# Attention with exponentials interleaved in SBUF: the two terms of a chunk alternate in pairs of queries instead of single queries

## The chip, the cores and the metric

The kernel runs on one NeuronCore of a Trainium2 chip. The metric is the device time of one execution in microseconds (us). Three timed executions of the kernel before gave 4507.30, 4506.31 and 4498.84 us; their median is 4506.31 us. Engines are named as in the profile: PE (TensorE), ACT (ScalarE), DVE (VectorE), POOL (GpSimd) and SP (SyncE, which issues most DMAs).

## What is computed

The input is two images of 256 channels on 64 x 64 positions, so 4096 tokens each. The reference has two layers. The first is a state-space block with an MLP (group norm, projections, a causal convolution, a scan over the tokens, an MLP); the change doesn't touch it. The second is an attention layer with eight heads of 32 channels over all 4096 tokens:

```python
qkv = jnp.einsum('bchw,oc->bohw', x, qkv_w) + qkv_b[None, :, None, None]
qkv = qkv.reshape(b, 3, num_heads, head_dim, n)
q, k, v = (qkv[:, 0], qkv[:, 1], qkv[:, 2])
attn_logits = jnp.einsum('bhci,bhcj->bhij', q, k) * scale
attn_weights = jax.nn.softmax(attn_logits, axis=-1)
out = jnp.einsum('bhij,bhcj->bhci', attn_weights, v)
...
x = x + _L1_conv_ref(_gn(x), L1_conv_qkv_w, L1_conv_qkv_b, 8)
```

Everything is float32. The kernel takes the exponentials without subtracting a maximum, and it divides by their sum at the end of each query tile. (A second, slower routine, `attention_any_range`, is run only if a sum has left the range of the numbers; here it is not run.)

## The kernel before, in words

The first layer fills roughly the first half of the span: a planner (`Plan`) orders its instructions by costs and due times. The attention that follows has an order written out by hand, in `attention`, and the change lies there alone.

**Tiles and slots.** Two images are worked one after the other. An image has two groups of four heads, a group has eight tiles of T = 512 queries, and a tile goes over the 4096 keys in NC = 32 pieces of P = 128 keys. One piece of one tile is a slot `s`; there are 2 x 2 x 8 x 32 = 1024 of them. The keys lie on the 128 partitions, the queries along the free axis. In a slot four things happen:

- `logits` (L1120 to L1134): PE makes the logits of four heads, two heads ("a half") per PSUM tile `s` of 128 x 1024; there are three such tiles.
- `exponentials` (L1136 to L1145): ACT takes the exponential of each half from PSUM to SBUF, 1024 elements per partition.
- `values` (L1155 to L1167): PE multiplies the exponentials with the values `v` and adds the product into the PSUM tile `po`. Each head takes a quarter of the array's columns. A float32 product is two matmul instructions, so that a slot has eight here.
- `add_up` (L1169 to L1194): the exponentials are also summed over the keys, for the softmax's divisor. Summing over the 32 slots is elementwise; only at the end of a tile does PE sum over the 128 partitions (`finish`, L1212).

`run` (L1231 to L1262) puts these in this order for slot `s`: the exponentials of `s`, the values of `s - 1`, a piece of the side work (`finish` of the tile before), the logits of `s + 1`, the sums of `s`. So PE's queue alternates between four logit matmuls and eight value matmuls. ACT's queue alternates between the two halves.

**How the sums are shared out.** Half 1 of every slot goes to a tile `e` of its own, contiguous, and is added by POOL (L1185, L1192, L1194) and partly by DVE (L1189, L1191). Half 0 of every slot but the tile's last one goes into a *chunk*, which takes several slots' terms, and DVE sums them with one `tensor_reduce` (`sum_chunk`, L1151 to L1153). A chunk has four places. `place(c)` says where piece `c` goes: the first chunk of a tile takes pieces 0 to 3; every later one takes three pieces in places 1 to 3, and its place 0 has the running sum, which the reduce of the chunk before it wrote there (L1177, L1178). That makes nine such reduces in a tile, and a tenth one (L1175), for pieces 28 to 30, writes the total to `acc_sb`. The last piece's half 0 goes to a contiguous `e` (L1143). Chunks come from a pool of two buffers.

**The chunk's layout, which the change is about.** Per partition a chunk is `[2 q, 2 h, T, 2 k]` in float32. Place `p` is `q = p // 2` and `k = p % 2`, `h` is the head within the half. So for one head and one `q`, the words in memory are: query 0 term k=0, query 0 term k=1, query 1 term k=0, query 1 term k=1, and so on. 16 bytes hold two queries of two terms. Three instructions touch it:

- ACT's exponential (L1144) writes one word, skips one, writes one.
- PE's value matmul (L1161) reads one word, skips one, reads one: 512 words at a step of 8 bytes.
- DVE's reduce (L1153) reads for each query two neighbouring words (k = 0, 1), then two neighbouring words 8 KB further on (q = 1), and writes one word: 4096 words in, 1024 out. For a running sum its output goes to every second word of the next chunk.

The chunk's tiles are also used as plain 2 x 1024 buffers when the second image is projected (L1023 to L1030).

## Time and profile before

| What | Value |
|---|---|
| Timed executions | 4498.84 to 4507.30 us, median 4506.31 us |
| Profiled execution, span from first to last instruction | 4505.2 us |
| Mean granted TensorE clock in it | 0.977 of full speed |
| Busy share of the span | PE 94%, DVE 86%, POOL 85%, ACT 84% |
| First value matmul of the attention to the last (L1161) | about 2119 to 4484 us |

The span is what is seen of the profiled execution; no other time is given for it. It is 1.1 us below the median of the timed ones. A profile line for a group of instructions has: source line, engine, operation, `output<-inputs` by the program's names, shapes, the count after an x, then the busy time of all in us, the mean of one in ns, then the idle time of that engine just before them, and what ended that wait. `PEld` is the loading of weights, which goes on beside the matmuls. "The chain that ended last" follows the program back from its last instruction, at each step to what released it.

### The profile page before, as it was taken

Reading aid. Unit: us, or ns where it says so; the run is one execution under the profiler, and the core shown is the slowest. Engines: PE = TensorE matmul, PEld = TensorE weight load, DVE = VectorE, ACT = ScalarE, POOL = GpSimd, SP = SyncE. Lnnn points to the kernel's source line nnn. Section 1 sums busy time; section 2 is a strip of 40 time slices with the busy share of each in tenths; the row PEclk is TensorE's granted clock in tenths of the full one; section 3 lists DMA queues with packets and bytes.
Section 4 is the critical chain, followed back from the end, with each engine's and each line's share of the span. In section 5 each row is a group of like instructions: output and inputs, shape, how many; then the busy total and the mean of one; then the engine's idle time right before and its main releaser. Section 6 shows DMA issues by size and latency. Waiting matters only on the chain.

```text
span 4505.2 us, 53942 instructions
## 1 busy us (share of the span) xinstructions
PE 4257.1 (94%) x18530; PEld 1642.2 (36%) x18530; DVE 3890.9 (86%) x3309; ACT 3768.4 (84%) x4842; POOL 3807.4 (85%) x2249
## 2 busy tenths in 40 slices
PE   5789999999999999988999999999999999999998
PEld 2233333333333333333333333333353333333333
DVE  4999999999999989894888888888848888888888
ACT  4788888888788889873999999999849999999997
POOL 2999999999999999994788888888728888888886
PEclk8899999999999999999999999999999999999999
DMA  5233333333443434445210140101091110401100
GB/s 192 94 120 101 110 125 122 127 127 127 143 148 134 139 126 140 147 153 144 58 27 17 29 101 17 26 17 30 24 265 35 46 26 17 101 17 29 27 19 8
DMA packets 172281, 389.23 MB, mean 86 GB/s; under 512 B 23392, under 2 KB 49760, under 8 KB 163808
## 3 DMA queue, kind: packets, MB, share of 16 engines
q1 hardware_dynamic: 171120, 383.37, 27.4%
q8 instruction: 147, 2.41, 0.2%
q10 hardware_dynamic: 880, 2.36, 0.2%
q14 instruction: 134, 1.10, 0.1%
HBM read 292.33 MB, written 93.32 MB: 86 GB/s over the span
## 4 chain that ended last, share of the span: by engine, by line
PE 57%; DVE 4%; ACT 3%; POOL 3%; issue 2%; DMA 1%; DVEq 0%; POOLq 0%; SPq 0%; ACTq 0%
PE s L1131 25%; PE po L1161 24%; PE mm L444 3%; DVE h L839 2%; POOL h L845 2%; ACT da L828 1%; ACT L244 1%; PE mm L677 1%; PE s L1016 1%; PE y L871 1%; POOL dbu L834 1%; PE sums_ps L1212 1%; DVE bn L834 1%; PE mm L641 0%; PE bn L444 0%
## 5 line engine op out<-in xcount | busy, mean ns | idle before, releaser
L1153 DVE TENSOR_REDUCE chunk<-chunk 128x1024 f32<-128x4096 f32 x288 | 1270.6, 4412 | 242.4 <-ACT chunk L1144 242.3
L1194 POOL TENSOR_TENSOR acc_p<-acc_p,e 128x1024 f32<-128x1024 f32 x480 | 1151.9, 2400 | 196.7 <-ACT e L1144 178.0
L1144 ACT ACTIVATE chunk<-s 128x1024 f32<-128x1024 f32 x992 | 1121.5, 1131 | 185.5 <-PE s L1131 139.9
L845 POOL TENSOR_TENSOR h<-h,c 128x1024 f32<-128x1024 f32 x512 | 1208.5, 2371 | 42.0 <-ACT state L842 28.9
L1131 PE MATMUL s<-q,k 128*128 128x512 f32 x4096 | 1228.4, 422 | 5.8 <-ACT chunk L1144 4.9
L1161 PE MATMUL po<-chunk,v 128*32 128x512 f32 x3968 | 1121.7, 642 | 0.0
L1161 PE MATMUL po<-e,v 128*32 128x512 f32 x4224 | 1080.0, 605 | 0.0
L1144 ACT ACTIVATE e<-s 128x1024 f32<-128x1024 f32 x1056 | 1072.7, 1019 | 7.4 <-PE s L1131 6.9
L1131 PEld LDWEIGHTS s<-q,k 128*128 128x128 f32 x4096 | 691.3, 188 | 1014.4 <-issue 915.0
L828 ACT ACTIVATE da<-dt_rep,neg_a 128x512 f32<-128x512 f32 x1024 | 690.5, 701 | 128.7 <-DVE h L839 106.0
L1192 POOL TENSOR_TENSOR acc_p<-acc_p,e 128x512 f32<-128x512 f32 x480 | 620.2, 1292 | 129.3 <-ACT e L1144 106.6
L839 DVE TENSOR_TENSOR_SCAN h<-da,state,dbu 128x512 f32<-128x512 f32 x512 | 650.5, 1273 | 42.8 <-POOL dbu L834 40.2
L839 DVE TENSOR_TENSOR_SCAN h<-da,state,bn 128x512 f32<-128x512 f32 x512 | 647.1, 1264 | 11.6
L834 POOL TENSOR_TENSOR dbu<-dtu_rep,b 128x512 f32<-128x512 f32 x384 | 488.5, 1283 | 19.7 <-DMA dtu_rep<-dtu_dram 15.0
L244 ACT ACT_TABLE_LOAD x332 | 426.0, 1283 | 6.7 <-PEq L1451 0.7
L444 PE MATMUL bn<-proj,pick 112*128 112x512 f32 x512 | 296.4, 595 | 112.2 <-DVE h L839 111.6
L871 PE MATMUL y<-h,sum 128*32 128x512 f32 x2048 | 359.1, 635 | 42.2 <-POOL h L845 42.1
L834 DVE TENSOR_TENSOR bn<-dtu_rep,bn 128x512 f32<-128x512 f32 x512 | 348.6, 681 | 41.4 <-PE bn L444 27.8
L1191 DVE TENSOR_TENSOR acc<-acc,e 128x512 f32<-128x512 f32 x448 | 310.7, 694 | 30.9 <-ACT e L1144 17.5
L1161 PEld LDWEIGHTS po<-chunk,v 128*32 128x32 f32 x3968 | 144.3, 108 | 361.5 <-issue 349.9
L444 PE MATMUL mm<-yn,w_in 128*128 128x512 f32 x512 | 254.7, 625 | 10.3 <-ACT yn L534 9.1
L444 PE MATMUL mm<-yn,w 128*128 128x512 f32 x512 | 246.5, 611 | 4.2 <-ACT hid L666 2.1
(143 smaller groups left out, 4016.3 us busy)
## 6 DMA issues: line engine op xcount, KB each, us to landing
dt_rep<-dt_dram SPq DMA_DIRECT2D x128, 512.0 KB, 5.1
dtu_rep<-dtu_dram SPq DMA_DIRECT2D x128, 512.0 KB, 5.7
k<-qk_dram SPq DMA_DIRECT2D x62, 512.0 KB, 7.3
q<-qk_dram SPq DMA_DIRECT2D x124, 256.0 KB, 4.7
b<-bc_dram SPq DMA_DIRECT2D x64, 256.0 KB, 3.0
c<-bc_dram SPq DMA_DIRECT2D x64, 256.0 KB, 3.7
dt_dram<-dt SPq DMA_DIRECT2D x64, 256.0 KB, 2.0
dtu_dram<-lw SPq DMA_DIRECT2D x64, 256.0 KB, 2.3
```

What stands on the lines that cost most here:

```text
L244: self.nc.scalar.preload_act_table_set(self.TABLES[task.table])
L444: nc.tensor.matmul(out, lhsT=lhsT, rhs=rhs, start=(i == 0), stop=(i == len(pairs) - 1))
L828: nc.scalar.activation(da[j].tile, dt.tile[:, j, :], AF.Exp, scale=scale)
L834: engine.tensor_mul(out.tile, dtu.tile[:, j, :], rows.tile)
L839: nc.vector.tensor_tensor_scan(h.tile[:, j, :], da[j].tile, dbu.tile, initial, ALU.mult, ALU.add)
L845: nc.gpsimd.tensor_tensor(h.tile, h.tile, rows_c.tile.unsqueeze(1).to_broadcast([P, 2, T]), ALU.mult)
L1131: nc.tensor.matmul(ps[:, j, :], lhsT=keys[i // NT, kt][:, h, kj : kj + P], rhs=queries[i][:, h, :], start=True, stop=True)
L1144: nc.scalar.activation(e, todo[s].s[half], AF.Exp, scale=SCALE)
L1153: nc.vector.tensor_reduce(out, terms, AX.XY, ALU.add)
L1161: nc.tensor.matmul(tiles[i].po[h * D : (h + 1) * D, :], lhsT=v[:, c, g * P + h * D : g * P + (h + 1) * D], rhs=todo[s].e[h // 2][:, h % 2, :],
L1192: nc.gpsimd.tensor_add(acc_p[:, 1, :], acc_p[:, 1, :], eb[:, 1, :])
L1194: nc.gpsimd.tensor_add(acc_p, acc_p, eb)
```

## The change

The chunk becomes `[2 q, 2 h, T/2, 2 k, 2 u]`, where `u` is the query within a pair. The words of one head and one `q` are now: query 0 term k=0, query 1 term k=0, query 0 term k=1, query 1 term k=1, then the next pair of queries. The same 16 bytes hold the same four values; the middle two have changed places.

```diff
     def chunk():
-        return ec.tile([P, 2, 2, T, 2], F32, name="chunk")
+        return ec.tile([P, 2, 2, T // 2, 2, 2], F32, name="chunk")
...
-        halves = chunk().rearrange("p q h t k -> p q (h t k)").rearrange("p q (m t) -> p q m t", t=T)
+        halves = chunk().rearrange("p q h t k u -> p q (h t k u)").rearrange("p q (m t) -> p q m t", t=T)
...
-                e = todo[s].chunk[:, k // 2, :, :, k % 2]
+                e = todo[s].chunk[:, k // 2, :, :, k % 2, :]
+                logit = todo[s].s[half].rearrange("p h (t u) -> p h t u", u=2)
             else:
                 e = ep.tile([P, 2, T], F32, name="e")
-            nc.scalar.activation(e, todo[s].s[half], AF.Exp, scale=SCALE)
+                logit = todo[s].s[half]
+            nc.scalar.activation(e, logit, AF.Exp, scale=SCALE)
...
         def sum_chunk(s, out):
-            terms = todo[s].chunk.rearrange("p q h t k -> p (h t) q k")
+            terms = todo[s].chunk.rearrange("p q h t k u -> p (h t) u q k")
             nc.vector.tensor_reduce(out, terms, AX.XY, ALU.add)
...
-                sum_chunk(s, tile_.acc[:, 0:2].rearrange("p h t -> p (h t)"))
+                sum_chunk(s, tile_.acc[:, 0:2].rearrange("p h (t u) -> p (h t) u", u=2))
             elif place(c) == 3:
                 todo["chunk"] = chunk()
-                sum_chunk(s, todo["chunk"].rearrange("p q h t k -> p q (h t) k")[:, 0, :, 0])
+                sum_chunk(s, todo["chunk"].rearrange("p q h t k u -> p q (h t) k u")[:, 0, :, 0])
```

So ACT writes two neighbouring words and skips two, PE reads two neighbouring words and skips two, and the reduce reads, for each query, two words 8 bytes apart (k = 0, 1), then two words 8 bytes apart in the other `q`; its outputs for two queries lie side by side. The value matmul's line itself (`todo[s].e[h // 2][:, h % 2, :]`) is unchanged; it follows the new shape of `e`.

## The prediction, made before the changed kernel was run

> **What bounds the kernel now.** I read the costliest groups first, to find the three instructions that touch a chunk, then the chain that ended last, then busy time by window, then the waits. The groups:

> ```profile
> L1153 DVE TENSOR_REDUCE chunk<-chunk 128x1024 f32<-128x4096 f32 x288 | 1270.6, 4412 | 242.4 <-ACT chunk L1144 242.3
> L1144 ACT ACTIVATE chunk<-s 128x1024 f32<-128x1024 f32 x992 | 1121.5, 1131 | 185.5 <-PE s L1131 139.9
> L1161 PE MATMUL po<-chunk,v 128*32 128x512 f32 x3968 | 1121.7, 642 | 0.0
> L1161 PE MATMUL po<-e,v 128*32 128x512 f32 x4224 | 1080.0, 605 | 0.0
> L1144 ACT ACTIVATE e<-s 128x1024 f32<-128x1024 f32 x1056 | 1072.7, 1019 | 7.4 <-PE s L1131 6.9
> ```

> Two pairs of rows do the same arithmetic and differ in the step of the operand in SBUF. An exponential into a chunk (every second word) takes 1131 ns, into the contiguous `e` 1019. A value matmul that reads a chunk takes 642 ns, one that reads `e` 605. The reduce takes 4412 ns for 4096 words, 1.08 ns a word all in. PE's value matmuls were idle before themselves for 0.0 us.

> The chain of waits in a piece of the attention, with start, length and what ran:

> ```profile
> 2544.99 1.13 PE s L1131 x4
> ...
> 2547.17 1.13 PE s L1131 x4
> 2548.30 1.06 PE po L1161 x6
> 2549.36 1.13 PE s L1131 x4
> 2550.49 0.99 PE po L1161 x8
> 2551.48 1.13 PE s L1131 x4
> ```

> The chain has nothing but PE in it: four logit matmuls, then the value matmuls, without a gap. A slot is the distance from one `s` row to the next. From 2544.99 to 2549.36 there are two slots of 2.185 us. The next, to 2551.48, takes 2.12. It is the slot whose value matmuls are of a tile's last piece, where both halves are contiguous (the row has eight, and 0.99 in place of 1.06). So PE pays 0.065 us in each slot that reads a chunk. That is the only price of the old layout that lies on the path.

> How near the others are, over two tiles (64 slots); columns are the window and busy us (count) for PE, weight loads, DVE, ACT and POOL, then clock and DMA:

> ```profile
> 2341.60:2483.00 141.40, 141.40 (x785) 53.77 (x784) 123.78 (x73) 129.35 (x129) 117.92 (x64) 1.00 0.09 23
> ```

> A tile takes 70.7 us and PE is busy in all of it (31 x 2.185 + 2.12 + 0.86 for the sums at its end, by the chain, is 70.7). DVE is busy 61.9 of it, ACT 64.7, POOL 59.0. And the waits of an attention stretch:

> ```profile
> DVE chunk L1153 <- ACT chunk L1144: 107.9, 90, 3.4
> ...
> ACT chunk L1144 <- PE s L1131: 65.3, 314, 1.0
> ```

> DVE waits for ACT, ACT for PE: both follow PE's pace. DVE has 70.7 - 61.9 = 8.8 us free per tile; over ten reduces that is 0.88 us each. A reduce may grow to 4.41 + 0.88 = 5.29 us before DVE sets the pace.

> [...] with two words per line ACT pays (1131 - 1019) / 1024 = 0.11 ns a word and PE 65 / 1024 = 0.06 ns a column (two rounds of 512 in a slot).

> [...]

> [...]

> **The change, part by part.** Comparing the two built programs, every engine has the same instructions in the same order with the same semaphores. Nothing is added, removed or moved, no queue is passed and no wait is added. Only the patterns of 992 exponentials, 3968 matmuls and 320 reduces (288 + 32 a tile's last) differ. So the sum has three terms.

> *ACT's write.* Two adjacent words, then two skipped. The number of 16-byte lines is the same (512), the number of 8-byte units is halved. Best case 1019 ns, a gain of 112 ns x 992 = 111 us of ACT[...]. On the path either is worth nothing: ACT waits for PE ahead of chunk writes (139.9 us in all). The cover is 70.7 - 64.7 = 6.0 us a tile, 0.19 us per chunk write. Value: 0.

> *PE's read.* Same pattern, 256 lines a matmul as before. If PE's price comes with each 8-byte unit, it goes: 0.065 x 992 = 64.5 us gained. If it comes with each line, it stays: 0. [...] One number speaks for the line. In the first layer 16 contiguous float32 matmuls of 512 columns follow one another in 6.87 us (the chain's `mm L677 x16`), 0.84 ns a column; with PE's 0.06 that is 1.80 ns for a line with two words. An exponential of 512 contiguous words takes 588 ns (L600), one of 1024 takes 1019, so 0.84 ns a word and 157 ns of start-up; a chunk write then has (1131 - 157) / 512 = 1.90 ns for a line. [...] I take 0 and keep both ends.

> *DVE's read.* Now no two consecutive words are adjacent: word 0, word 2, a hop of 8 KB, word 0, word 2. By lines nothing changes[...] And ACT and PE, taking single words at 8 bytes' step, lose 7 to 13%[...]. I take 4.41[...]. Its writes (now side by side) are one word in four read and can't matter.

> Sum: 0 + 0 + 0. Against the profile's own span of 4505.2 that is 4505.2; the timed median is 1.1 us higher. Forecast **4506 us**, by itself 4497 to 4517 (the lower edge is the bound of no change[...]).

> **The rivals.**

> *PE is relieved* (faster). PE's price belongs to 8-byte units; slots fall to 2.12. For it: PE is the bound and nothing else is within 6 us a tile; then ACT's 64.7 and DVE's 61.9 still fit under 68.7. Against it: the equal figure per line. Time: 4506 - 64.5 = 4442, or between the two if a part stays.

> *The reduce becomes the bound* (slower). The place is L1153 and the price is the loss of adjacency in its reads; it decides from 5.29 us per reduce. [...] The chunks' two buffers carry it on: a slow reduce holds its chunk, behind it in DVE's queue stand the sums of L1191 and the end of a tile, ACT's next chunk waits for the buffer, and PE for ACT. [...] Both effects could meet: PE relieved and DVE at about 5.1 would still gain the whole 64 us.

> *The change does nothing of what it says* is excluded by the built program: the patterns are there.

> **How the numbers follow.** No effect, 0.28 (within 0.2% of the median, 9 us, about what a measurement of this kernel can tell from no change: 0.24; 0.02 faster, 0.02 slower). PE relieved, whole: 0.22; in part, 4450 to 4497: 0.12. Reduce slower, mildly (4517 to 4620): 0.18; heavily[...]: 0.20. So faster 0.36, same 0.24, slower 0.40. The likeliest single case is no effect. Leaving out the heavy case would leave out just 0.20 and the edges more, so the range takes in its price: from 4436 (4442 less 0.005 us of reading error in a slot, times 992) to 5125[...].

> **What would show it.** In the changed profile: `po<-chunk` at 642 means the line pays, 605 the 8-byte unit. The slot in the chain: 2.185 or 2.12. `TENSOR_REDUCE chunk<-chunk` at 4412 or from 5.3 us up; in the last case DVE appears in the chain and ACT's chunk writes wait for DVE. The exponential into a chunk at 1131 or 1019 tells the same of a write and should move with PE's. I am wrong if PE's rows and ACT's fall together, or if the reduce's row rises.

## The result, and the profile after

The changed kernel takes 4502.80 us (median of 12 runs, 4498.94 to 4510.81), the kernel before 4506.28 us in 12 runs beside it. The ratio is 1.000 with a 95% interval of 0.9993 to 1.0008: no difference that can be measured, as forecast (4506, by itself 4497 to 4517). The profiled execution has a span of 4500.9 us.

These five groups of the kernel after answer to the five of before. Line numbers are two higher from L1144 on; columns as before, count, then busy us and mean ns, then idle time ahead.

```profile
L1155 DVE TENSOR_REDUCE chunk<-chunk 128x1024 f32<-128x4096 f32 x288 | 1270.5, 4412 | 241.2 <-ACT chunk L1146 241.1
...
L1146 ACT ACTIVATE chunk<-s 128x1024 f32<-128x1024 f32 x992 | 1119.6, 1129 | 187.9 <-PE s L1131 144.7
...
L1163 PE MATMUL po<-chunk,v 128*32 128x512 f32 x3968 | 1121.7, 643 | 0.0
L1163 PE MATMUL po<-e,v 128*32 128x512 f32 x4224 | 1079.8, 605 | 0.0
L1146 ACT ACTIVATE e<-s 128x1024 f32<-128x1024 f32 x1056 | 1072.0, 1018 | 7.3 <-PE s L1131 6.9
```

The reader is to see that no mean moved by more than 2 ns: 4412 and 4412, 1131 and 1129, 642 and 643. All three patterns changed, and each instruction takes what it took. The chain in the same stretch of the kernel after (start, length, what ran):

```profile
2546.33 1.13 PE s L1131 x4
2547.46 1.06 PE po L1163 x6
2548.52 1.13 PE s L1131 x4
2549.64 0.99 PE po L1163 x8
2550.64 1.13 PE s L1131 x4
```

A slot that reads a chunk takes 2548.52 - 2546.33 = 2.19 us, the one that reads none 2.12. The difference of before (2.185 against 2.12) is still there, as far as the chain's hundredths show it.

This settles that nothing happened, not why. Either the price belongs to something that both layouts share, or two effects cancel. My theory (the "line theory" of what follows) was that an engine's time goes by the 16-byte lines it comes to, and that both layouts take two words from each. A "line" is four neighbouring words, counted in fours from the start of an unmoved chunk. That 16 bytes are a unit which counts was my assumption, and for it I had only the prediction's estimate from PE's and ACT's rows; the runs below test it. The rivals: the unit is 8 bytes and the pattern's second dimension took back what the pairs gave; or PE and ACT pay for sharing a buffer with DVE and not for a step. A "visit" below is a stretch of words that an engine takes from one line before it goes to another.

### The profile page after: what moved, and what is told of

It reads as the page before. It is cut to its first block, busy times and chain, and to the rows that moved or that the text cites. A ratio compares the mean times of both kernels' runs of the same rounds, so it can differ in the third digit from the quotient of the medians.

```text
span 4500.9 us, 53942 instructions
## 1 busy us (share of the span) xinstructions
PE 4252.5 (94%) x18530; PEld 1638.1 (36%) x18530; DVE 3889.7 (86%) x3309; ACT 3768.4 (84%) x4842; POOL 3810.6 (85%) x2249
## 4 chain that ended last, share of the span: by engine, by line
PE 65%; POOL 12%; DVE 8%; issue 6%; ACT 5%; DMA 3%; SPq 0%; POOLq 0%; DVEq 0%; ACTq 0%
PE s L1131 25%; PE po L1163 24%; PE mm L444 8%; POOL h L845 7%; DVE h L839 5%; POOL dbu L834 4%; PE y L871 2%; PE mm L677 2%; ACT L244 2%; ACT da L828 2%; PE mm L641 1%; DVE bn L834 1%; PE bn L444 1%; POOL dt L615 1%; POOL lw L614 1%
## 5 line engine op out<-in xcount | busy, mean ns | idle before, releaser
L1155 DVE TENSOR_REDUCE chunk<-chunk 128x1024 f32<-128x4096 f32 x288 | 1270.5, 4412 | 241.2 <-ACT chunk L1146 241.1
L1146 ACT ACTIVATE chunk<-s 128x1024 f32<-128x1024 f32 x992 | 1119.6, 1129 | 187.9 <-PE s L1131 144.7
L1131 PE MATMUL s<-q,k 128*128 128x512 f32 x4096 | 1227.8, 422 | 7.3 <-ACT chunk L1146 6.4
L1163 PE MATMUL po<-chunk,v 128*32 128x512 f32 x3968 | 1121.7, 643 | 0.0
L1131 PEld LDWEIGHTS s<-q,k 128*128 128x128 f32 x4096 | 690.0, 188 | 1016.7 <-issue 915.4
```

The lines of the kernel that those rows point to most:

```text
L1131: nc.tensor.matmul(ps[:, j, :], lhsT=keys[i // NT, kt][:, h, kj : kj + P], rhs=queries[i][:, h, :], start=True, stop=True)
L1146: nc.scalar.activation(e, logit, AF.Exp, scale=SCALE)
L1155: nc.vector.tensor_reduce(out, terms, AX.XY, ALU.add)
L1163: nc.tensor.matmul(tiles[i].po[h * D : (h + 1) * D, :], lhsT=v[:, c, g * P + h * D : g * P + (h + 1) * D], rhs=todo[s].e[h // 2][:, h % 2, :],
```

## The experiments

**The reduce reads one word per visit.** The changed kernel with the two summed axes swapped, so that it goes back and forth between two places 8 KB apart.

```diff
-            terms = todo[s].chunk.rearrange("p q h t k u -> p (h t) u q k")
+            terms = todo[s].chunk.rearrange("p q h t k u -> p (h t) u k q")
```

> The changed kernel with the reduce's two summed axes swapped: per query it reads word 0, then word 0 of the other q 8 KB on, then word 2, then word 2 there, so each visit to a 16-byte line takes one word. All of the sum is computed. Line theory[...]: the reduce goes from 4412 to about 7200 ns, DVE becomes the bound, about 5110 us; the exponential into a chunk and the value matmuls keep 1129 and 643 ns on their own. Rival (DVE doesn't care for lines or neighbours in this reduce at all): 4412 ns and 4503 us.

Measured: 4510.29 us, ratio 1.0012 (1.0003 to 1.0020).

```profile
L1155 DVE TENSOR_REDUCE chunk<-chunk 128x1024 f32<-128x4096 f32 x288 | 1320.8, 4586 | 210.8 <-ACT chunk L1146 210.1
```

The reduce takes 4586 ns, not 7200, a number with no run behind it: the expectation of the line theory failed here for DVE. Two accounts were left, and a later pair of runs decides between them: what costs is the number of lines visited in turn, and two are few enough (theory A); or a hop of 8 KB costs nothing, whatever the number (theory B). The 0.17 us cost something nevertheless. This is what PE's value matmuls waited for at the start of a tile, in the kernel before and then in this one (total us, times, longest):

```profile
PEld po L1161 <- DVE po_sb L1202: 10.9, 30, 0.4
```

```profile
PEld po L1163 <- DVE po_sb L1204: 15.5, 30, 0.5
```

The first value matmul of a tile needs `po` free, and DVE's copy of `po` (in `finish`) stands in DVE's queue behind a reduce. The wait grew by 4.6 us, most of the 4.9 that the kernel lost against the runs of before beside it (4505.42). From the sums matmuls of one tile to those of the next it is 70.92 us in this kernel and 70.76 in the kernel before; over 30 tiles that is 4.8 us.

**Runs of four queries**, 16 bytes, so that ACT and PE take whole lines and the reduce meets four lines per query.

```diff
-        return ec.tile([P, 2, 2, T // 2, 2, 2], F32, name="chunk")
+        return ec.tile([P, 2, 2, T // 4, 2, 4], F32, name="chunk")
...
-                logit = todo[s].s[half].rearrange("p h (t u) -> p h t u", u=2)
+                logit = todo[s].s[half].rearrange("p h (t u) -> p h t u", u=4)
...
-                sum_chunk(s, tile_.acc[:, 0:2].rearrange("p h (t u) -> p (h t) u", u=2))
+                sum_chunk(s, tile_.acc[:, 0:2].rearrange("p h (t u) -> p (h t) u", u=4))
```

> Runs of four queries (16 bytes, one whole line) in place of two. All of the sum is computed. Line theory: PE and ACT now take four words from each line they come to, so the value matmul from a chunk goes from 643 to 605 ns and the exponential into a chunk from 1129 to 1019; the reduce takes one word per visit (two lines side by side, then two lines 8 KB on) and goes to about 7200 ns, so that DVE bounds the kernel at about 5110 us[...]. Rival (it is the pattern's second dimension, runs and gaps, that costs PE and ACT as much as the pairs saved them): 643 and 1129 ns stay.

Measured: 5387.21 us, ratio 1.196 (1.194 to 1.198). The groups of this kernel:

```profile
L1155 DVE TENSOR_REDUCE chunk<-chunk 128x1024 f32<-128x4096 f32 x288 | 2176.2, 7556 | 184.8 <-ACT chunk L1146 184.6
...
L1146 ACT ACTIVATE chunk<-s 128x1024 f32<-128x1024 f32 x992 | 1020.4, 1029 | 1166.3 <-DVE chunk L1155 678.8 <-PE s L1131 486.5 <-DMA qk_dram<-chunk 0.2
```

The exponential into a chunk now takes 1029 ns, near the 1019 of a contiguous one in the kernel before, and the reduce goes to 7556 ns. In the idle column ACT now waits for the reduce (678.8 us), for a buffer of the chunk. PE's mean (658 ns) says nothing here: PE waits 238.7 us ahead of these matmuls, the granted clock of the profiled run is 0.918, and the matmuls that read the contiguous `e` have risen as well, from 605 to 660 ns; the run with the light reduce below has it clean.

**Contiguous terms**, four of 4 KB each. This edit is against the kernel before.

```diff
-        return ec.tile([P, 2, 2, T, 2], F32, name="chunk")
+        return ec.tile([P, 2, 2, 2, T], F32, name="chunk")
...
-                e = todo[s].chunk[:, k // 2, :, :, k % 2]
+                e = todo[s].chunk[:, k // 2, k % 2]
...
-            terms = todo[s].chunk.rearrange("p q h t k -> p (h t) q k")
+            terms = todo[s].chunk.rearrange("p q k h t -> p (h t) q k")
```

> The four terms of a chunk each contiguous, 4 KB apart; the reduce reads one word from each. All of the sum is computed. Line theory: value matmul from a chunk 605 ns, exponential 1019 ns, the reduce one word per visit, about 7200 ns and 5110 us in all (4412 ns and 4439 us if hops of 4 KB are free). Rival (PE and ACT pay for sharing a buffer that DVE and each other are using, not for the step): 643 and 1129 ns stay although the step is gone.

Measured: 5367.30 us, ratio 1.191 (1.189 to 1.193).

```profile
L1153 DVE TENSOR_REDUCE chunk<-chunk 128x1024 f32<-128x4096 f32 x288 | 2168.3, 7529 | 179.3 <-ACT chunk L1144 179.2
...
L1144 ACT ACTIVATE chunk<-s 128x1024 f32<-128x1024 f32 x992 | 1018.2, 1026 | 1150.2 <-DVE chunk L1153 641.2 <-PE s L1131 502.8 <-DVE sums L1215 3.1
```

So with four lines visited in turn, one word each, the reduce takes 7529 / 4096 = 1.84 ns a word all in, against 4412 / 4096 = 1.08 in the kernel before.

**One word per line for ACT and PE**, four terms side by side for the reduce. This edit, too, is against the kernel before.

```diff
-        return ec.tile([P, 2, 2, T, 2], F32, name="chunk")
+        return ec.tile([P, 2, T, 2, 2], F32, name="chunk")
...
-                e = todo[s].chunk[:, k // 2, :, :, k % 2]
+                e = todo[s].chunk[:, :, :, k // 2, k % 2]
...
-            terms = todo[s].chunk.rearrange("p q h t k -> p (h t) q k")
+            terms = todo[s].chunk.rearrange("p h t q k -> p (h t) q k")
```

> The four terms of a query side by side: the reduce reads 4096 words in a row, ACT writes and PE reads every fourth word, one in each 16-byte line. All of the sum is computed. Line theory: a round of value matmuls from a chunk takes 512 x 1.8 = 0.92 us in place of 0.47, the slot 2.187 + 0.90 = 3.1 us; the exponential 157 + 1024 x 1.85 = 2050 ns; the reduce 4412; in all about 4503 + 992 x 0.90 = 5400 us. Rival (the unit is 8 bytes, and at a step of 8 bytes each word already has its own): 643 and 1129 ns stay, 4503 us.

Measured: 5383.15 us, ratio 1.195 (1.193 to 1.197). Three groups of it:

```profile
L1144 ACT ACTIVATE chunk<-s 128x1024 f32<-128x1024 f32 x992 | 2035.9, 2052 | 197.9 <-PE s L1131 156.6 <-DMA qk_dram<-chunk 0.2
L1161 PE MATMUL po<-chunk,v 128*32 128x512 f32 x3968 | 1992.6, 1091 | 0.0
L1153 DVE TENSOR_REDUCE chunk<-chunk 128x1024 f32<-128x4096 f32 x288 | 1272.9, 4420 | 788.0 <-ACT chunk L1144 788.0
```

2052 ns where 2050 were expected and 5383 us where 5400 were. PE stays the bound, and its timeline gives the slot (start us, length, instruction):

```profile
2601.38 1.20 PE L1131 MATMUL s<-q,k 128*128 128x512 f32 x4
...
2604.44 1.20 PE L1131 MATMUL s<-q,k 128*128 128x512 f32 x4
```

3.06 us, 0.94 more than a contiguous slot. The rival of an 8-byte unit is out: by it this kernel would have cost nothing. The reduce writes each running sum to a line of its own here and still takes 4420 ns; in the kernel before, with writes at a step of 8 bytes, it takes 4412. So no price of that step is seen here.

**The number of lines in turn, or hops of 8 KB free?** The axes swapped, as in the first experiment, in the contiguous kernel and in the one with runs of four.

```diff
-            terms = todo[s].chunk.rearrange("p q k h t -> p (h t) q k")
+            terms = todo[s].chunk.rearrange("p q k h t -> p (h t) k q")
```

> Contiguous terms again, but the reduce's two summed axes swapped: for each query 0, 8, 4, 12 KB instead of 0, 4, 8, 12 KB. All of the sum is computed. With the axes swapped in the changed kernel a reduce that goes back and forth between two lines 8 KB apart took 4586 ns and not the 7200 expected. Theory A[...]: four lines are visited in turn,[...] the reduce stays at about 7530 ns, 5367 us. Theory B (what is free is the 8 KB hop itself[...]): three of four hops are then of 8 or 12 KB and one of 4 KB, at most about 5300 ns, and with PE's rows at 605 about 4445 us.

> Runs of four queries with the reduce's axes swapped: line, line 8 KB on, next line, its fellow 8 KB on. All of the sum is computed. Theory A[...]: four lines in turn, about 7550 ns and 5387 us. Theory B (8 KB hops free): about 4500 to 5300 ns and about 4445 us.

Measured: 5366.23 us, ratio 1.191 (1.189 to 1.193), and 5384.01 us, ratio 1.195 (1.193 to 1.197). The reduces, contiguous first:

```profile
L1153 DVE TENSOR_REDUCE chunk<-chunk 128x1024 f32<-128x4096 f32 x288 | 2167.2, 7525 | 178.6 <-ACT chunk L1144 178.4
...
L1155 DVE TENSOR_REDUCE chunk<-chunk 128x1024 f32<-128x4096 f32 x288 | 2172.6, 7544 | 188.9 <-ACT chunk L1146 188.7
```

The other order of the hops changes the reduce by 4 ns in the one (7529 before the swap) and by 12 in the other (7556). Theory B, which had at most 5300, falls; theory A, with 7530 and 7550, fits. At one word per visit, two lines in turn take 4586 ns and four take 7525 to 7556. No run here has three lines in turn, and why the number counts was not shown.

**PE's price alone.** To see what PE's reading is worth on the path, the reduce is made light: it reads one term of four, which leaves three quarters of half 0's terms out of the divisor. First in the contiguous kernel, then in the changed one, then with runs of four.

```diff
-            nc.vector.tensor_reduce(out, terms, AX.XY, ALU.add)
+            nc.vector.tensor_reduce(out, terms[:, :, 0:1, 0:1], AX.XY, ALU.add)
```

(With pairs or runs `terms` has one axis more.)

> Contiguous terms, and each reduce reads one term of the four (1024 words), so three quarters of half 0's sum are left out and DVE is far from being the bound. Line theory: PE reads four words per line, slots of 2.122 us throughout, value matmul from a chunk 605 ns, exponential 1019; 992 x 0.065 = 64.5 us less than before, about 4440 us. Rival (PE's price comes from DVE or ACT being in the same buffer, or PE meets another wait 65 us on): 4503 us.

> Control for the one before: the changed kernel with the reduce reading one term of four (three quarters of half 0's sum left out). PE's reading is as in the changed kernel. Line theory: 643 and 1129 ns (the latter nearer 1115 with the reduce gone for most of the time), slots of 2.187 us, no change, 4503 us. Rival (PE and ACT are slowed by the long reduce): the rows fall towards 605 and 1019 and the time towards 4440.

> Runs of four queries, each a whole 16-byte line, with the reduce reading one term of four (three quarters of half 0's sum left out). Line theory: as with contiguous terms, slots of 2.122 us, 605 and about 1024 ns, 4441 us. Rival (a pattern of runs and gaps has a price of its own): between 605 and 643 ns, 4441 to 4503 us.

Measured: contiguous 4441.51 us, ratio 0.9857 (0.9841 to 0.9874); pairs 4501.78, 0.9992 (0.9983 to 1.0001); runs of four 4436.51, 0.9846 (0.9829 to 0.9862). First the two rows of the contiguous one, then of the pairs, then of the runs:

```profile
L1161 PE MATMUL po<-chunk,v 128*32 128x512 f32 x3968 | 1045.1, 605 | 0.0
L1144 ACT ACTIVATE chunk<-s 128x1024 f32<-128x1024 f32 x992 | 1016.5, 1025 | 207.7 <-PE s L1131 111.0 <-ACT e L1144 59.0 <-DMA qk_dram<-chunk 0.2
```

```profile
L1146 ACT ACTIVATE chunk<-s 128x1024 f32<-128x1024 f32 x992 | 1115.7, 1125 | 192.2 <-PE s L1131 94.1 <-ACT e L1146 54.9 <-DMA qk_dram<-chunk 0.2
L1163 PE MATMUL po<-chunk,v 128*32 128x512 f32 x3968 | 1121.5, 642 | 0.0
```

```profile
L1163 PE MATMUL po<-chunk,v 128*32 128x512 f32 x3968 | 1044.8, 605 | 0.0
...
L1146 ACT ACTIVATE chunk<-s 128x1024 f32<-128x1024 f32 x992 | 1019.7, 1028 | 203.3 <-PE s L1131 109.7 <-ACT e L1146 57.7 <-DMA qk_dram<-chunk 0.2
```

Relieving DVE alone gives nothing measurable (pairs). Whole lines for PE give 63 us (contiguous, against 4504.53 for before) and 67 us (runs of four, against 4503.48), where 992 x 0.065 = 64.5 were expected. And runs with gaps cost PE no more than contiguous words (605 and 605): the rival of the second dimension is out. The sharing of the buffer is out as well: with most of DVE's reading gone the pairs still take 642 and 1125 ns, and with all of it the contiguous kernel's exponential into a chunk took 1026.

**The same runs astride two lines.** The runs of four with the light reduce, the whole chunk two words on.

```diff
-        return ec.tile([P, 2, 2, T // 4, 2, 4], F32, name="chunk")
+        words = ec.tile([P, 8 * T + 4], F32, name="chunk")[:, 2 : 2 + 8 * T]
+        return words.rearrange("p (q h t k u) -> p q h t k u", q=2, h=2, k=2, u=4)
```

> The same runs of four queries, moved by two words, so that each run lies astride two 16-byte lines, two words in each; the reduce reads one term of four as before (three quarters of half 0's sum left out). Line theory (what counts is words per 16-byte line, and the lines are fixed in memory): two words per line again, 643 and 1118 to 1129 ns, slots of 2.187 us, 4503 us. Rival (what counts is the length of a run of neighbouring words, wherever it lies): 605 and 1024 ns, 4441 us, as in the run beside it.

```profile
L1164 PE MATMUL po<-chunk,v 128*32 128x512 f32 x3968 | 1117.6, 641 | 275.7 <-ACT chunk L1147 275.7
L1147 ACT ACTIVATE chunk<-s 128x1024 f32<-128x1024 f32 x992 | 1101.2, 1110 | 498.7 <-PE s L1132 428.0 <-DVE chunk L1156 68.8
```

The rows are near those of two words per line, 641 and 1110 ns (643 and 1118 to 1129 were expected), although each run still has four neighbouring words. The expected 4503 us were missed: the kernel takes 4871.10 us (ratio 1.081, 1.079 to 1.083). That time can't be compared, because the moved buffer changed more than the addresses. The page counts 54423 instructions where the runs of four on whole lines have 54097, and the value matmuls wait for exponentials into a chunk (275.7 us in the first row; 0.0 in the run before). Neither theory is about that wait, and why this build has it stays open. Where there is no such wait, a slot is two lines' slot (start, length, instruction):

```profile
2601.28 1.20 PE L1132 MATMUL s<-q,k 128*128 128x512 f32 x4
...
2603.45 1.20 PE L1132 MATMUL s<-q,k 128*128 128x512 f32 x4
```

2.17 us, against 2.12 with the same runs on whole lines.

**Pairs on odd words.** The changed kernel with the whole chunk one word on (as above, with offset 1 and u=2).

> The changed kernel with the whole chunk moved by one word, so that the pairs start on odd words. All of the sum is computed. Line theory[...]: PE and ACT still take two words from every line they come to and stay at 643 and 1129 ns; the reduce finds every other query's terms astride (four lines with one word each),[...] about 5900 ns; DVE is then the bound, 4700 to 4850 us. Rival (DVE's reduce only minds how often it hops to the far q, or nothing about lines): 4412 ns, 4503 us.

Measured: 4551.37 us, ratio 1.0100 (1.0083 to 1.0117), where 4700 to 4850 were expected.

```profile
L1156 DVE TENSOR_REDUCE chunk<-chunk 128x1024 f32<-128x4096 f32 x288 | 1315.3, 4567 | 211.1 <-ACT chunk L1147 210.5
...
L1147 ACT ACTIVATE chunk<-s 128x1024 f32<-128x1024 f32 x992 | 1119.6, 1129 | 189.4 <-PE s L1132 163.1
L1164 PE MATMUL po<-chunk,v 128*32 128x512 f32 x3968 | 1118.9, 642 | 2.4
```

PE's 642 and ACT's 1129 ns are as expected; the reduce takes 4567 ns where I expected about 5900. The loss lies outside the tiles of the attention, which take 70.8 us in both. It is in the projection of the second image (from the first sums matmul of the last tile before it to that of the first tile after it 203.5 us, in the changed kernel 153.8), where ACT waits for stores of the chunk's buffers:

```profile
ACT chunk L1027 <- DMA qk_dram<-chunk: 103.8, 16, 15.8
```

In the changed kernel the same wait is 13.2 us, over 6 times. Both builds with a moved buffer have it long (107.0 us with the runs astride); what in the move causes it was not looked for. The reduce itself did not slow as expected: 4567 ns. The 5900 was my estimate: for every other query it took the time per word of four lines in turn, from the contiguous kernel's 7529 ns. This run doesn't show that price here. Why this reduce and the one with a word per visit take 155 and 174 ns more than 4412 stays open.

No kernel here that computes everything beats the two. 4437 to 4442 us is what PE would allow, but whole lines for PE mean four lines per query for this reduce, and DVE has no time for that: 7525 to 7556 ns were measured, where by the prediction's estimate 5290 fit.

## Why the prediction was right, step by step

- *PE bounds, with 0.065 us per slot for the chunk's step.* Right, and it is on the path: with that price gone and DVE kept out of the way, 4441.51 us against the 4442 of the rival "PE is relieved". That rival had the right price and the wrong owner, the 8-byte unit.
- *PE's and ACT's terms, 0 because the lines are the same.* Right, and now shown by taking four, two and one word per line. PE: 605, 643, 1091 ns. ACT: 1028, 1129, 2052. What decided it was an estimate from the trace of before: near-equal times for two words, 1.80 ns for PE and 1.90 for ACT. With 1.85 ns, between the two, for one word per line, 2050 ns were expected of the exponential and 2052 measured. One reading behind it was wrong: L600, from which the 157 ns of start-up come, is a logarithm and not an exponential. The result doesn't hang on it: the one-word exponential comes to 512 lines more than that of before and takes 2052 - 1131 = 921 ns more. What was an argument from near-equal numbers is now measured. The moved runs show that the place of the words counts, not the length of the run alone: the same four words take PE 605 ns on a whole line and 641 astride two.
- *DVE's term, 4.41 us.* Right in size (4412). That each visit still takes two words, as the line theory has it, is not shown to be the reason. One word per visit, with only two lines in turn, costs just 4% more (4586), so the fact that the changed layout, too, goes between only two lines might have been enough. No run has two words per visit and four lines in turn, which would tell the two reasons apart. To that extent the term came out by luck.
- *The reduce becomes the bound, from 5.29 us.* It did not happen in the changed kernel; where the experiments made it happen, my sums were too kind. The point: at 4586 ns the tile's end already waits longer (4.6 us more in all), since the average slack is not the slack of the moment. The price: for 7529 ns the formula gives 4506 + (7.53 - 5.29) x 320 = 5223, measured 5367. A tile of the contiguous kernel takes 98.7 us, where the formula has 61.9 + 10 x (7.53 - 4.41) = 93.1. In a window of 141.40 us that kernel's DVE is busy for 134.49, so DVE is the bound with gaps of its own:

```profile
2341.60:2483.00 141.40, 113.56 (x558) 41.74 (x550) 134.49 (x54) 86.06 (x91) 83.98 (x47) 0.88 0.05 14
```

The contiguous kernel's rows say what the gaps are: ahead of its reduces DVE waits 179.2 us for ACT, 5.6 a tile, and ACT waits 641.2 us for DVE. With two buffers of the chunk each waits for the other by turns. The prediction named that wait and put no time on it.

- *The chances.* "Slower" had the largest sum, 0.40, on the assumption that the reduce needs adjacent words. It doesn't here: the changed kernel has none, and its reduce takes 4412 ns, as with adjacent words. The trace of before had spoken against it (PE and ACT, with single words at a step of 8 bytes, take 642 against 605 ns and 1131 against 1019), and more weight there would have been earned.

## What to carry to other kernels

Before changing an interleaved layout, count for each engine how many words it takes from each 16-byte line per visit. Here four took PE 605 and ACT 1028 ns (contiguous words 605 and 1019), two 642 and 1131, one 1091 and 2052. Swapping words inside the line changed no count here, and no time beyond 2 ns of an instruction. When one engine's words per line went up in these layouts, another's went down; price that one too, and by its queue at the tightest moment, not by its average slack.
